# LSTM with residual on one core: the initial state's product goes into the x bank, and TensorE forms the second remainder of four of the eight weight parts with diagonal matrices

## The chip, the cores and the metric

The kernel runs on one core of a Trainium2 chip. The metric is the device time of one execution in microseconds (us); the median of three executions of the kernel before is 2270.43 us (2269.09 to 2270.66). Times of instructions come from one profiled execution, which took 2270.51 us as a whole and whose program spans 2268.2 us in the trace. All times below that say "at 44.78" are counted from the start of that span.

## What is computed

An LSTM layer runs over 512 time steps for a batch of 16, with 512 inputs and 512 hidden units; its output is added to the input.

```python
xW = jnp.einsum('ntd,dg->ntg', x, Wx) + b
def step(carry, xw_t):
    prev_h, prev_c = carry
    a = xw_t + prev_h @ Wh
    i = jax.nn.sigmoid(a[:, :Hdim])
    f = jax.nn.sigmoid(a[:, Hdim:2 * Hdim])
    o = jax.nn.sigmoid(a[:, 2 * Hdim:3 * Hdim])
    g = jnp.tanh(a[:, 3 * Hdim:])
    next_c = f * prev_c + i * g
    next_h = o * jnp.tanh(next_c)
    return ((next_h, next_c), next_h)
c0 = jnp.zeros_like(h0)
_, hs = jax.lax.scan(step, (h0, c0), jnp.swapaxes(xW, 0, 1))
x = x + jnp.swapaxes(hs, 0, 1)
```

x is (16, 512, 512), h0 is (16, 512), Wx and Wh are (512, 2048), all float32.

## The kernel before, in words

**Two stages.** A start prepares the weights and does step 0; then a loop (L519) does the 512 steps. All five engines' orders are written out by hand: each engine runs its instructions strictly in the order in which the program records them, and waits at the first one that is not ready. GpSimd (POOL) and SyncE (SP) issue the transfers, and their queues are in program order too.

**One step of the loop.** The list STEP_PE (L23) orders TensorE's work of a step: twelve products (q3aa to q3bb, 96 matmuls with 128x256 float16 moving data, line L210) and half of a projection of x two pairs of steps ahead (x0, x1: line L187, float32, 16 trace records). The list STEP (L24) orders the work of VectorE (DVE) and ScalarE (ACT): transposing the gates out of PSUM (turn, turno), folding two partial sums (fold, foldo), tanh and sigmoid, the new cell and the new h in float16 parts (p1, copy, p2, p2r, tile `parts`). The letters a and b stand for the two halves of the hidden units. The bank `gates` collects the products of one step and half; `seed` (L196) writes x's projection from bank `xb` into it before the products are added.

**The weights in parts.** The loop's products are float16. Therefore Wh is scaled by a power of two and split at the start into three float16 terms wq[0], wq[1], wq[2], in eight pieces n = 0 to 7 (piece n holds row block n // 2 and column half n % 2, 128x1024 each; pieces 0 to 3 belong to half a of the rows, 4 to 7 to half b). The scale needs the largest magnitude of each half: `bound` (L430) reduces it from the loaded weights, on DVE by a reduction, on ACT by an Abs with accumulation; `scales` (L444) turns it into powers of two. `split(n, k)` (L463) then makes five operations for each piece:

- k=0, wq[0] = scaled weights (ACT, L469; for pieces 6 and 7 DVE, L471)
- k=1, r1 = weights times scale minus wq[0] (DVE, L474)
- k=2, wq[1] = r1 (ACT, L478)
- k=3, r2 = r1 - wq[1] (DVE, L481)
- k=4, wq[2] = r2 times 4096 (ACT, L483)

**Step 0.** The initial state h0 is transposed to hT0 (L501) and multiplied with the float32 weights: `first_products` (L219), 64 matmuls of 128 columns into the gates banks, which have been seeded before; the loop's first pass runs them, and then the element work of step 0. Step 1 is the first that needs `parts` and the split weights; its first product is on the record at 44.78.

**Transfers.** SP issues the eight loads of Wh (L377), the eight of Wx (L388), then the rest of the first block of x and the second block (L151). POOL issues the four of h0 (L382) and then 24 for the first three pairs of steps of x (`load_first`, L156). A transfer's semaphore is used again eight transfers later, and the issue waits for the earlier landing. `turn_x` (L173) waits with one small copy (`seen`, L179) for the transfers of a group of pairs, and transposes x of one pair; before the first projection it waits for all three pairs.

**Banks.** There are four banks of gates (two halves, even and odd steps) and four of xb. TensorE first fills the gates with zeros (L407) and xb with the bias (L418); ACT copies the bias from xb[0] (L428).

Of the kernel before, what the change touches and what calls it, by code (L numbers as in the profile page):

```python
# [24 lines left out]
    "turn_a turno_a fold_a tanh_a foldo_a sig_a turn_b sigo_a scale_a mix_a fold_b "  # L25
    "tanh_b cell_a ctanh_a turno_b foldo_b sig_b p1_a sigo_b h_a copy_a mix_b p2_a "
    "scale_b cell_b rem_a ctanh_b p2r_a p1_b h_b copy_b p2_b rem_b p2r_b"
)


@with_exitstack
def lstm_residual(ctx: ExitStack, tc: tile.TileContext, x, h0, wx, wh, b, out):
# [68 lines left out]
    wq = [const.tile([P, NK, G * H], HP, tag=f"wq{i}", name=f"wq{i}") for i in range(3)]  # L101

    wx_j = wx_sb.rearrange("p k (g c j u) -> p k j g c u", g=G, c=NK, j=NJ)
    wh_j = wh_sb.rearrange(
        "p k (e g h c j u) -> p k e h j g c u", e=2, g=2, h=2, c=2, j=NJ
    )
    wq_j = [
        w.rearrange("p k (g h c j u) -> p k h j g c u", g=G, h=2, c=2, j=NJ) for w in wq
    ]
    bias = const.tile([P, G * P], FP, tag="bias", name="bias")  # L110
    mask = const.tile([P, S2], FP, tag="mask", name="mask")
    zero = const.tile([1, G * P], HP, tag="zero", name="zero")
    amax = const.tile([P, 5], FP, tag="amax", name="amax")
    top = const.tile([P, 2], FP, tag="top", name="top")
    bits = const.tile([P, 2, 2], FP, tag="bits", name="bits")
    sc = const.tile([P, 2, 4], FP, tag="sc", name="sc")
    S, RS, RS2, RSL = ([sc[:, h, i : i + 1] for h in range(2)] for i in range(4))


# [33 lines left out]
                        in_=x_j[j, :, s * XB + i0 * S2 + r : (s + 1) * XB : S2, c],  # L153
                    )

    def load_first(i1):  # L156
        xs[0] = xsp.tile([P, XP, P], FP, tag="xs", name="xs_0")
        for i in range(i1):
            for j in range(NJ):
                for r in range(S2):  # L160
                    p0 = j * Q + r * N
                    nc.gpsimd.dma_start(
                        out=xs[0][p0 : p0 + N, i].rearrange("p (c u) -> p c u", c=NK),
                        in_=x_j[j, :, i * S2 + r],
                    )
# [6 lines left out]

    def turn_x(q):  # L173
        s, i = divmod(q, XP)
        if i == 0 or q == FIRST:

            a, e = (0, FIRST) if q == 0 else (i, XP)
            seen = tmp.tile([P, XP, NK], FP, tag="seen", name=f"seen_{q}")
            nc.vector.tensor_copy(  # L179
                seen[:, a:e], xs[s].rearrange("p i (c u) -> p i c u", c=NK)[:, a:e, :, 0]  # L180
            )
        xT[q] = xtp.tile([P, NK, Q], FP, tag="xT", name=f"xT_{q}")
        nc.vector.transpose(xT[q].rearrange("p c m -> p (c m)"), xs[s][:, i])  # L183

    def project(q, c):
        for j in range(NJ):
            nc.tensor.matmul(  # L187
                xb[q % NXB][j * Q : (j + 1) * Q],
                lhsT=xT[q][:, c],
                rhs=wx_j[:, c, j],  # L190
                start=False,
                stop=False,
                skip_group_check=True,
            )

    def seed(t, h):  # L196
        nc.scalar.mul(  # L197
            gates[h][t % 2][:, :GU].rearrange("p (g u) -> p g u", g=G),
            xb[t // 2 % NXB].rearrange("p (g h u) -> p h g u", g=G, h=2)[:, h],
            mask[:, t % 2 : t % 2 + 1],  # L200
        )
# [14 lines left out]
                    skip_group_check=True,  # L216
                )

    def first_products(kh, h, hT):  # L219
        for cc in range(2):  # L220
            for e in range(2):
                for j in range(NJ):
                    nc.tensor.matmul(
                        gates[h][0][j * Q : (j + 1) * Q, (1 - e) * P : (2 - e) * P],
                        lhsT=hT[:, 2 * kh + cc],
                        rhs=wh_j[:, 2 * kh + cc, e, h, j],
                        start=False,
                        stop=False,
                        skip_group_check=True,
                    )  # L230


    gc = [state.tile([P, 2, 2 * N], FP, tag=f"gc{h}", name=f"gc{h}_init") for h in range(2)]
# [140 lines left out]
    for c in range(NK):  # L374
        for e in range(2):
            f = slice(e * GH, (e + 1) * GH)
            nc.sync.dma_start(out=wh_sb[:, c, f], in_=wh[c * P : (c + 1) * P, f])  # L377
    nc.vector.memset(zero, 0.0)
    nc.vector.memset(h_in, 0.0)
    nc.vector.memset(ones, 1.0)  # L380
    for j in range(NJ):
        nc.gpsimd.dma_start(  # L382
            out=h_in[j * Q : j * Q + N].rearrange("p (c u) -> p c u", c=NK), in_=h0_j[j]
        )
    load_first(FIRST)
    for c in range(NK):
        for e in range(2):
            nc.sync.dma_start(  # L388
# [38 lines left out]
                )  # L427
    nc.scalar.copy(bias, xb[0])  # L428

    def bound(i, c, on_act, f=slice(0, G * H)):  # L430
# [12 lines left out]

    def scales(h):  # L444


        nc.vector.tensor_reduce(
            top[:, h : h + 1], amax[:, 3 * h : 3 + 2 * h], mybir.AxisListType.X, ALU.max
        )
        t = top[:, h : h + 1].bitcast(I32)  # L450
        e, inv = bits[:, h, 0:1], bits[:, h, 1:2]
        nc.vector.tensor_scalar(
            inv.bitcast(I32), t, EXP, EXP, ALU.bitwise_and, ALU.bitwise_xor
        )
        nc.vector.tensor_scalar(e.bitcast(I32), t, EXP, None, ALU.bitwise_and)
        nc.vector.tensor_scalar(RS2[h], inv, 2.0**12, 0.5, ALU.mult, ALU.min)
        nc.vector.tensor_scalar(RS[h], inv, 2.0**13, 1.0, ALU.mult, ALU.min)
        nc.vector.tensor_scalar(S[h], e, 2.0**-14, 1.0, ALU.mult, ALU.max)
        nc.vector.tensor_scalar(RSL[h], RS[h], 1.0 / LO, None, ALU.mult)

    r1, r2 = {}, {}

    def split(n, k):  # L463
# [4 lines left out]
        if k == 0 and n < 6:  # L468
            nc.scalar.mul(f[0], w, RS2[c // 2])  # L469
        elif k == 0:  # L470
            nc.vector.tensor_scalar(f[0], w, RS2[c // 2], None, ALU.mult)  # L471
        elif k == 1:
            r1[n] = tmp.tile([P, GH], FP, tag="r1", name=f"r1_{n}")
# [3 lines left out]
        elif k == 2:  # L477
            nc.scalar.copy(f[1], r1[n])  # L478
        elif k == 3:
            r2[n] = tmp.tile([P, GH], FP, tag="r2", name=f"r2_{n}")  # L480
            nc.vector.tensor_tensor(r2[n], r1[n], f[1], ALU.subtract)  # L481
        else:
            nc.scalar.mul(f[2], r2[n], LO)  # L483

    NH = 2 * NK
    bound(0, 0, False)
    bound(1, 1, True, slice(0, GH))
    bound(2, 1, False, slice(GH, 2 * GH))
    scales(0)
    split(0, 0)  # L490
    split(0, 1)
    split(1, 0)
    for n in range(NH):
        if n == 1:
            bound(3, 2, False)
            bound(4, 3, True)
            scales(1)
        if n == 2:
            for q in range(FIRST):
                turn_x(q)  # L500
            nc.vector.transpose(hT0.rearrange("p c m -> p (c m)"), h_in)  # L501
            for q in range(2):
                for c in range(NK):
                    project(q, c)
        if n + 1 < NH:
            split(n + 1, 1)
        split(n, 2)
        split(n, 3)
        if n:
            split(n - 1, 4)  # L510
        if n + 2 < NH:
            split(n + 2, 0)
        if n == 5:
            for t in range(2):
                for h in range(2):
                    seed(t, h)
    split(NH - 1, 4)

    for t in range(T):  # L519
        s, ti = divmod(t, XB)  # L520
        q, half = divmod(t + 4, 2)
        if ti == 0:
            hist[s] = outp.tile([P, XP, NK, Q], FP, tag="hist", name=f"hist_{s}")

        for op in STEP_PE.split():
            if op[0] == "x":
                if q < NP:
                    project(q, 2 * half + int(op[1:]))
            elif t:
                products(t, int(op[1]), "ab".index(op[2]), "ab".index(op[3]))  # L530
            elif op[1] == "3":
                first_products("ab".index(op[2]), "ab".index(op[3]), hT0)

        for op in STEP.split():
            name, h = op.split("_")
            act(t, name, "ab".index(h))

        if t + 2 < T:
            seed(t + 2, 0)
        if t % 2:  # L540
            for h in range(2):
                unscale(t // 2, h)
            if q + 1 < NP:
                turn_x(q + 1)
        else:
            if t and q + 1 < NP:
                put_bias(q + 1)
            if t:
                residual(t // 2 - 1)
        if t + 2 < T:  # L550
            seed(t + 2, 1)
        if ti == 0 and s + 2 < NS:
            load_xs(s + 2)
# [29 lines left out]
```

## Time and profile before

| what | us |
|---|---|
| median of three executions | 2270.43 |
| the profiled execution | 2270.51 |
| its span in the trace | 2268.2 |
| busy in the span: TensorE matmuls / VectorE / ScalarE / GpSimd | 2234.5 / 1957.2 / 1839.7 / 131.1 |
| first product of step 1 (L210) | at 44.78 |
| first product of step 2, by the chain of waits | at 50.60 |
| one step later on, 2.62 of products and 1.72 of projection | 4.34 |
| stretch without a matmul before the first projection | 17.4 |

The profile's page lists for each engine busy time and share, then the span in 40 slices, the transfer queues, the chain of work that ended last, and groups of instructions (line, engine, operation, output and inputs, count, busy us, mean ns, idle time before them and what ended it). The timeline gives instructions in order of time: start in us, duration or extent of a merged run in us, engine, line, operation, output and inputs, count, and in brackets the engine's idle time before it and the releaser. The chain of waits in order of time gives start, length and what was on the chain. PE is TensorE, DVE VectorE, ACT ScalarE. A float32 matmul of the program leaves two matmul records.

### The profile page before, as it was taken

Reading aid. Unit: us, or ns where it says so; the run is one execution under the profiler, and the core shown is the slowest. Engines: PE = TensorE matmul, PEld = TensorE weight load, DVE = VectorE, ACT = ScalarE, POOL = GpSimd, SP = SyncE. Lnnn points to the kernel's source line nnn. Section 1 sums busy time; section 2 is a strip of 40 time slices with the busy share of each in tenths; the row PEclk is TensorE's granted clock in tenths of the full one; section 3 lists DMA queues with packets and bytes.
Section 4 is the critical chain, followed back from the end, with each engine's and each line's share of the span. In section 5 each row is a group of like instructions: output and inputs, shape, how many; then the busy total and the mean of one; then the engine's idle time right before and its main releaser. Section 6 shows DMA issues by size and latency. Waiting matters only on the chain.

```text
span 2268.2 us, 138001 instructions
## 1 busy us (share of the span) xinstructions
PE 2234.5 (99%) x57444; PEld 1466.8 (65%) x57444; DVE 1957.2 (86%) x11853; ACT 1839.7 (81%) x7959; POOL 131.1 (6%) x287
## 2 busy tenths in 40 slices
PE   6999999999999999999999999999999999999997
PEld 3666666666666666666666666666666666666665
DVE  7888888888888888888888888888888888888887
ACT  6888888888888888888888888888888888888887
POOL 2000000000000000000000000000000000000000
PEclk9999999999999999999999999999999999999999
DMA  5011111111111111111111111111111111111001
GB/s 166 16 22 23 16 17 16 22 22 19 17 17 19 22 22 16 17 17 22 23 18 16 17 20 23 22 16 17 16 23 22 19 16 17 20 22 21 15 9 17
DMA packets 297716, 50.93 MB, mean 22 GB/s; under 512 B 294593, under 2 KB 295041, under 8 KB 297089
## 3 DMA queue, kind: packets, MB, share of 16 engines
q1 hardware_dynamic: 295872, 41.85, 11.4%
q8 instruction: 450, 7.37, 1.4%
q14 instruction: 176, 1.44, 0.2%
q0 software_dynamic: 896, 0.23, 0.1%
q10 hardware_dynamic: 322, 0.04, 0.0%
HBM read 25.21 MB, written 16.78 MB: 19 GB/s over the span
## 4 chain that ended last, share of the span: by engine, by line
PE 97%; DMA 1%; DVE 1%; issue 0%; ACT 0%; POOL 0%; SPq 0%; POOLq 0%; DVEq 0%
PE gates L210 59%; PE xb L187 38%; DMA xs<-in_x_dram 1%; DVE r L481 0%; DMA h_in<-in_cond_dram 0%; DVE r L474 0%; ACT wq L483 0%; SPq L347 0%; POOL h_in L382 0%; DMA out_dram<-ob 0%; DVE wq L471 0%; DVE xT L183 0%; POOLq L578 0%; DVE pr L290 0%; POOL ob L359 0%
## 5 line engine op out<-in xcount | busy, mean ns | idle before, releaser
L210 PEld LDWEIGHTS <-parts 128*32 128x32 f16 x49056 | 1224.7, 96 | 442.2 <-DVE parts L306 306.0
L210 PE MATMUL gates<-wq,parts 128*32 128x256 f16 x49056 | 1427.4, 273 | 7.0 <-DVE parts L306 7.0
L187 PE MATMUL xb<-wx_sb,xT 128*32 128x512 f32 x8192 | 966.7, 593 | 17.4 <-DMA xs<-in_x_dram 17.4
L246 DVE STREAM_TRANSPOSE gt<-gates 128x192 f32<-128x192 f32 x1024 | 392.0, 383 | 216.2 <-PE gates L210 168.1
L187 PEld LDWEIGHTS xb<-wx_sb,xT 128*32 128x32 f32 x8192 | 235.4, 110 | 344.1 <-issue 340.3
L197 ACT ACTIVATE gates<-xb,mask 128x256 f32<-128x256 f32 x1024 | 451.3, 441 | 0.0
L280 ACT ACTIVATE gc<-pre 128x32 f32<-128x32 f32 x1022 | 234.6, 230 | 259.7 <-DVE pre L253 248.3
L288 ACT ACTIVATE os<-so,sc 128x32 f32<-128x32 f32 x1024 | 329.6, 322 | 16.7
L310 ACT COPY parts<-parts 128x32 f16<-128x32 f16 x1022 | 214.3, 210 | 132.2 <-DVE parts L306 132.2
L253 DVE SCALAR_TENSOR_TENSOR pre<-gt 128x96 f32<-128x96 f32 x1024 | 255.1, 249 | 0.0
L282 ACT ACTIVATE sif<-pre 128x64 f32<-128x64 f32 x1024 | 244.9, 239 | 0.0
L359 POOL TENSOR_TENSOR ob<-hb,xs 128x128 f32<-128x128 f32 x255 | 116.5, 457 | 2121.6 <-DVE hb L357 2039.4
L246 DVE STREAM_TRANSPOSE gto<-gates 128x64 f32<-128x64 f32 x1024 | 231.2, 226 | 0.0
L286 ACT ACTIVATE so<-preo 128x32 f32<-128x32 f32 x1024 | 227.0, 222 | 0.0
L298 ACT ACTIVATE tch<-gc 128x32 f32<-128x32 f32 x1024 | 226.8, 221 | 0.1
L320 DVE SCALAR_TENSOR_TENSOR parts<-rem,parts 128x32 f16<-128x32 f32 x1022 | 195.9, 192 | 35.5
L253 DVE SCALAR_TENSOR_TENSOR preo<-gto 128x32 f32<-128x32 f32 x1024 | 193.6, 189 | 17.5
L312 DVE SCALAR_TENSOR_TENSOR parts<-parts,hist 128x32 f16<-128x32 f16 x1022 | 193.3, 189 | 17.7
L290 DVE TENSOR_TENSOR pr<-sif,gc 128x64 f32<-128x64 f32 x1022 | 205.8, 201 | 0.0
L306 DVE TENSOR_TENSOR parts<-os,tch 128x32 f16<-128x32 f32 x1022 | 196.9, 193 | 0.0
L296 DVE TENSOR_TENSOR gc<-pr 128x32 f32<-128x32 f32 x1024 | 193.3, 189 | 0.0
L300 DVE SCALAR_TENSOR_TENSOR hist<-os,tch 128x32 f32<-128x32 f32 x1024 | 190.2, 186 | 0.3 <-ACT tch L298 0.3
(49 smaller groups left out, 740.1 us busy)
## 6 DMA issues: line engine op xcount, KB each, us to landing
xs<-in_x_dram SPq DMA_DIRECT2D x992, 16.0 KB, 2.1
out_dram<-ob SPq DMA_DIRECT2D x992, 16.0 KB, 1.6
wh_sb<-in_L_cond_Wh_dram SPq DMA_DIRECT2D x8, 512.0 KB, 7.8
wx_sb<-in_L_cond_Wx_dram SPq DMA_DIRECT2D x8, 512.0 KB, 11.7
out_dram<-ob SPq DMA_DIRECT2D x60, 8.0 KB, 1.5
xs<-in_x_dram SPq DMA_DIRECT2D x32, 10.0 KB, 2.3
xs<-in_x_dram POOLq DMA_DIRECT2D x24, 8.0 KB, 5.2
h_in<-in_cond_dram POOLq DMA_DIRECT2D x4, 8.0 KB, 6.0
```

Of the source, the lines that this page charges most:

```text
L187: nc.tensor.matmul(xb[q % NXB][j * Q : (j + 1) * Q], lhsT=xT[q][:, c], rhs=wx_j[:, c, j], start=False, stop=False, skip_group_check=True,)
L197: nc.scalar.mul(gates[h][t % 2][:, :GU].rearrange("p (g u) -> p g u", g=G), xb[t // 2 % NXB].rearrange("p (g h u) -> p h g u", g=G, h=2)[: ...
L210: nc.tensor.matmul(g[j * Q : (j + 1) * Q, :GU], lhsT=a[:, cc, k * N : (k + 2) * N], rhs=wq_j[i - 1][:, 2 * kh + cc, h, j], start=False, st ...
L246: nc.vector.transpose(gt.rearrange("p b m -> p (b m)"), gates[h][t % 2][:, b0 * Q : b1 * Q])
L253: nc.vector.scalar_tensor_tensor(pre.rearrange("p g (c n) -> p (g c) n", c=2), gt[:, :, (1 - t % 2) * N : (2 - t % 2) * N], 1.0 / LO, gt[: ...
L280: nc.scalar.activation(gc[h][:, 0], v["pre", h][:, 0], AF.Tanh)
L282: nc.scalar.activation(new("sif", t, h, [P, 2, 2 * N]), v["pre", h][:, 1:3], AF.Sigmoid)
L286: nc.scalar.activation(new("so", t, h, [P, 2 * N]), v["preo", h][:, 0], AF.Sigmoid)
L288: nc.scalar.mul(new("os", t, h, [P, 2 * N]), v["so", h], S[h])
L290: nc.vector.tensor_tensor(new("pr", t, h, [P, 2, 2 * N]), v["sif", h], gc[h], ALU.mult)
L298: nc.scalar.activation(new("tch", t, h, [P, 2 * N]), gc[h][:, 1], AF.Tanh)
L310: nc.scalar.copy(slots(t, h, 2), slots(t, h, 0))
```

## The change

Only the start and the first pass of the loop change; STEP_PE, STEP and the loop from step 1 stay as they are.

- **Order.** A list START replaces the nested order of the start and the loop's step 0. Each entry is one operation: b (bound), S (scales), hT, H (first product with row block c), xT (turn_x), P.q.c (project), seed, q1/q2/q3 (the three float16 terms; the suffix s is ACT, v is DVE), r1/r2, d1/d2/d3 (diagonal matmuls), and step 0's element operations. The loop begins at step 1.
- **h0's product.** `first_products` writes to xb[0], beside x's projection, as 32 matmuls of 256 columns instead of 64 of 128 into the gates; step 0's seeds then read the sum.
- **The second remainder on TensorE.** For pieces 0, 1, 2 and 4 (BY_PE, which names the gates banks used) r1 and r2 are not made on DVE. Instead DVE makes wq[1] directly in float16 (one operation), and TensorE makes the remainder in two gates banks: +scale diagonal times the float32 weights (d1, `rows`), minus-one diagonal times wq[0] (d2) and times wq[1] (d3, `neg16`), each as two matmuls of 512 columns with a full 128x128 stationary operand. ACT reads the two banks and writes wq[2] (q3).
- **The diagonal.** POOL makes `neg` with a memset and an affine_select, after h0's transfers and the first eight of x, ahead of the other sixteen of x. DVE copies it to `neg16`, ahead of the transposition of h0 and of the bounds, and makes `rows` at the end of each `scales`. In the built program POOL's library-configuration instruction, which was ahead of the first residual addition (L359), stands between the memset and the affine_select; on DVE the copy to `neg16` is the first instruction after the initial memsets.
- **Bounds.** Block 0 is bounded by ACT as a whole, block 1 by DVE in two pieces, blocks 2 and 3 by ACT; the maxima have eight columns, cleared first.
- **x.** The three first pairs are waited for one by one.

```diff
+BY_PE = {0: 1, 1: 0, 2: 1, 4: 0}
+START = (
+    "hT b.0.s H.0 b.1a.v b.1b.v H.1 S.0 q1.1.v d1.1 q1.2.s q1.3.v b.2.s q2.1.v d1.0 "
+    "q1.0.v b.3a.s r1.3 d2.1 d2.0 b.3b.s H.2 q2.0.v q2.3.s d3.1 S.1 q3.1.s d3.0 H.3 "
+    "xT.0 r2.3 q1.4.s d1.4 q1.7.s xT.1 q2.4.v P.0.0 q3.3.s r1.7 d2.4 q1.5.s d3.4 P.0.1 "
+    "q2.2.v q3.0.s P.1.0 r1.5 q2.7.s P.1.1 q3.4.s r2.7 P.0.2 q1.6.s P.1.2 q2.5.v q3.7.s "
+    "P.0.3 xT.2 r1.6 d1.2 seed.0.0 seed.0.1 turn_a q2.6.s turno_a turn_b fold_a turno_b "
+    "d2.2 fold_b tanh_a foldo_a sig_a foldo_b r2.6 d3.2 tanh_b sigo_a sigo_b sig_b "
+    "P.1.3 q3.2.s mix_a mix_b P.2.0 cell_a cell_b r2.5 scale_a ctanh_a ctanh_b scale_b "
+    "P.2.1 seed.1.0 seed.1.1 p1_a h_a h_b copy_a p1_b q3.5.s p2_a rem_a rem_b p2r_a "
+    "q3.6.v copy_b p2_b p2r_b seed.2.0 seed.2.1"
+)
...
+    def first_products(c):
+        for e in range(2):
+            for j in range(NJ):
+                nc.tensor.matmul(
+                    xb[0][j * Q : (j + 1) * Q, (1 - e) * GU : (2 - e) * GU],
+                    lhsT=hT0[:, c],
+                    rhs=wh_j[:, c, e, j],
...
-    load_first(FIRST)
+    load_first(0, 1)
+    nc.gpsimd.memset(neg, 0.0)
+    nc.gpsimd.affine_select(
+        out=neg, in_=neg, compare_op=ALU.not_equal, fill=-1.0, base=0,
+        pattern=[[-1, P]], channel_multiplier=1,
+    )
+    load_first(1, FIRST)
...
+    nc.vector.tensor_copy(neg16, neg)
...
+        nc.vector.tensor_scalar(rows[h], neg, RS[h], -1.0, ALU.mult, ALU.mult)
...
+        if op[0] == "d":
+            i = int(op[1])
+            for m in range(2):
+                g = slice(m * G * P, (m + 1) * G * P)
+                nc.tensor.matmul(
+                    gates[m][BY_PE[n]],
+                    lhsT=rows[c // 2] if i == 1 else neg16,
+                    rhs=w[:, g] if i == 1 else f[i - 2][:, g],
+                    start=(i == 1),
+                    stop=(i == 3),
+                    skip_group_check=True,
+                )
+        elif op == "q3" and n in BY_PE:
+            for m in range(2):
+                cast(on_act, f[2][:, m * G * P : (m + 1) * G * P], gates[m][BY_PE[n]], LO)
+        elif op == "q2" and n in BY_PE:
+            nc.vector.scalar_tensor_tensor(f[1], w, RS[c // 2], f[0], ALU.mult, ALU.subtract)
+        elif op == "q1":
+            cast(on_act, f[0], w, RS2[c // 2])
...
+    hist[0] = outp.tile([P, XP, NK, Q], FP, tag="hist", name="hist_0")
+    for op in START.split():
+        start(*op.split("."))
+    load_xs(2)
-    for t in range(T):
+    for t in range(1, T):
```

More of the change, by code (lines that the diff above doesn't have):

```diff
@@ L103, in lstm_residual @@
     wx_j = wx_sb.rearrange("p k (g c j u) -> p k j g c u", g=G, c=NK, j=NJ)
-    wh_j = wh_sb.rearrange(
-        "p k (e g h c j u) -> p k e h j g c u", e=2, g=2, h=2, c=2, j=NJ
-    )
+    wh_j = wh_sb.rearrange("p k (e g c j u) -> p k e j g c u", e=2, g=2, c=NK, j=NJ)
     wq_j = [
@@ L112, in lstm_residual @@
     zero = const.tile([1, G * P], HP, tag="zero", name="zero")
-    amax = const.tile([P, 5], FP, tag="amax", name="amax")
+    amax = const.tile([P, 8], FP, tag="amax", name="amax")
     top = const.tile([P, 2], FP, tag="top", name="top")
@@ L116, in lstm_residual @@
     sc = const.tile([P, 2, 4], FP, tag="sc", name="sc")
+    neg = const.tile([P, P], FP, tag="neg", name="neg")
+    neg16 = const.tile([P, P], HP, tag="neg16", name="neg16")
+    rows = [const.tile([P, P], FP, tag=f"rows{h}", name=f"rows{h}") for h in range(2)]
     S, RS, RS2, RSL = ([sc[:, h, i : i + 1] for h in range(2)] for i in range(4))
@@ L154, in load_xs, with load_first @@
                     )
-    def load_first(i1):
-        xs[0] = xsp.tile([P, XP, P], FP, tag="xs", name="xs_0")
-        for i in range(i1):
+    def load_first(i0, i1):
+        if i0 == 0:
+            xs[0] = xsp.tile([P, XP, P], FP, tag="xs", name="xs_0")
+        for i in range(i0, i1):
             for j in range(NJ):
@@ L174, in turn_x @@
         s, i = divmod(q, XP)
-        if i == 0 or q == FIRST:
-            a, e = (0, FIRST) if q == 0 else (i, XP)
+        if i == 0 or q <= FIRST:
+            a, e = (i, i + 1 if q < FIRST else XP)
             seen = tmp.tile([P, XP, NK], FP, tag="seen", name=f"seen_{q}")
@@ L217, in products @@
                 )
[L219 to L230, printed above, removed]
+    def first_products(c):
[5 more added lines that the diff above has]
+                    rhs=wh_j[:, c, e, j],
+                    start=False,
+                    stop=False,
+                    skip_group_check=True,
+                )
     gc = [state.tile([P, 2, 2 * N], FP, tag=f"gc{h}", name=f"gc{h}_init") for h in range(2)]
@@ L378, in lstm_residual @@
     nc.vector.memset(zero, 0.0)
+    nc.vector.memset(amax, 0.0)
     nc.vector.memset(h_in, 0.0)
@@ L384, in lstm_residual @@
         )
-    load_first(FIRST)
+    load_first(0, 1)
+    nc.gpsimd.memset(neg, 0.0)
+    nc.gpsimd.affine_select(
+        out=neg,
+        in_=neg,
+        compare_op=ALU.not_equal,
+        fill=-1.0,
+        base=0,
+        pattern=[[-1, P]],
+        channel_multiplier=1,
+    )
+    load_first(1, FIRST)
     for c in range(NK):
@@ L428, in lstm_residual, with bound @@
     nc.scalar.copy(bias, xb[0])
-    def bound(i, c, on_act, f=slice(0, G * H)):
+    nc.vector.tensor_copy(neg16, neg)
+    def bound(piece, on_act):
+        c = int(piece[0])
+        i = 2 * c + (piece[-1] == "b")
+        f = slice(0, 2 * GH) if len(piece) == 1 else slice((i % 2) * GH, (i % 2 + 1) * GH)
         w = wh_sb[:, c, f]
@@ L447, in scales @@
         nc.vector.tensor_reduce(
-            top[:, h : h + 1], amax[:, 3 * h : 3 + 2 * h], mybir.AxisListType.X, ALU.max
+            top[:, h : h + 1], amax[:, 4 * h : 4 * h + 4], mybir.AxisListType.X, ALU.max
         )
@@ L459, in scales, with cast, split @@
         nc.vector.tensor_scalar(RSL[h], RS[h], 1.0 / LO, None, ALU.mult)
+        nc.vector.tensor_scalar(rows[h], neg, RS[h], -1.0, ALU.mult, ALU.mult)
     r1, r2 = {}, {}
-    def split(n, k):
+    def cast(on_act, out, in_, scale):
+        if on_act:
+            nc.scalar.mul(out, in_, scale)
+        else:
+            nc.vector.tensor_scalar(out, in_, scale, None, ALU.mult)
+    def split(op, n, on_act):
         c, e = divmod(n, 2)
@@ L467, in split @@
         f = [q[:, c, (1 - e) * GH : (2 - e) * GH] for q in wq]
[L468 to L473, printed above, removed]
+        if op[0] == "d":
[8 more added lines that the diff above has]
+                    stop=(i == 3),
+                    skip_group_check=True,
+                )
+        elif op == "q3" and n in BY_PE:
[5 more added lines that the diff above has]
+            cast(on_act, f[0], w, RS2[c // 2])
+        elif op == "r1":
+            r1[n] = tmp.tile([P, GH], FP, tag="r1", name=f"r1_{n}", bufs=4)
             nc.vector.scalar_tensor_tensor(
@@ L476, in split @@
             )
-        elif k == 2:
-            nc.scalar.copy(f[1], r1[n])
-        elif k == 3:
+        elif op == "q2":
+            (nc.scalar.copy if on_act else nc.vector.tensor_copy)(f[1], r1[n])
+        elif op == "r2":
             r2[n] = tmp.tile([P, GH], FP, tag="r2", name=f"r2_{n}")
@@ L482, in split, with start @@
         else:
[L483 to L500, printed above, removed]
-            nc.vector.transpose(hT0.rearrange("p c m -> p (c m)"), h_in)
[L502 to L517, printed above, removed]
-    for t in range(T):
+            cast(on_act, f[2], r2[n], LO)
+    def start(op, a="", b=""):
+        if op == "b":
+            bound(a, b == "s")
+        elif op == "S":
+            scales(int(a))
+        elif op == "hT":
+            nc.vector.transpose(hT0.rearrange("p c m -> p (c m)"), h_in)
+        elif op == "xT":
+            turn_x(int(a))
+        elif op == "H":
+            first_products(int(a))
+        elif op == "P":
+            project(int(a), int(b))
+        elif op == "seed":
+            seed(int(a), int(b))
+        elif "_" in op:
+            name, h = op.split("_")
+            act(0, name, "ab".index(h))
+        else:
+            split(op, int(a), b == "s")
+    hist[0] = outp.tile([P, XP, NK, Q], FP, tag="hist", name="hist_0")
[3 more added lines that the diff above has]
+    for t in range(1, T):
         s, ti = divmod(t, XB)
@@ L528, in lstm_residual @@
                     project(q, 2 * half + int(op[1:]))
-            elif t:
+            else:
                 products(t, int(op[1]), "ab".index(op[2]), "ab".index(op[3]))
-            elif op[1] == "3":
-                first_products("ab".index(op[2]), "ab".index(op[3]), hT0)
         for op in STEP.split():
@@ L545, in lstm_residual @@
         else:
-            if t and q + 1 < NP:
+            if q + 1 < NP:
                 put_bias(q + 1)
-            if t:
-                residual(t // 2 - 1)
+            residual(t // 2 - 1)
         if t + 2 < T:
```

## The prediction

> **What bounds the kernel now.** I read the page first, then the chain of waits in order of time, then the timeline of the first 50 us.
>
> ```profile
> span 2268.2 us, 138001 instructions
> PE 97%; DMA 1%; DVE 1%; issue 0%; ACT 0%; POOL 0%; SPq 0%; POOLq 0%; DVEq 0%
> ```
>
> TensorE is 97% of the chain. The loop is bound by it, and the change leaves the loop alone. So only what lies ahead of TensorE's unbroken run can move. The chain of waits (start, length, what) shows where that begins:
>
> ```profile
> 3.23 6.58 DMA h_in<-in_cond_dram
> ...
> 21.48 5.21 DMA xs<-in_x_dram
> ...
> 26.96 0.17 DVE seen L179
> ...
> 40.00 2.35 DVE r L481 x2
> ...
> 42.37 1.06 ACT wq L483
> ...
> 44.78 4.10 PE gates L210 x93
> 48.88 1.72 PE xb L187 x16
> 50.60 2.62 PE gates L210 x93
> 53.22 1.72 PE xb L187 x15
> ```
>
> From 3.23 to 26.7 POOL's transfers are the chain, each waiting for an older landing; DVE then sits in `seen`. From 27 to 42.4 it is mostly DVE's remainders, at 44.78 step 1 begins. Its products take 4.10 where step 2's take 2.62: the granted clock is 0.67 between 44.8 and 48.9, after TensorE was idle from 42.0 to 44.8. From 48.88 on a step is 2.62 + 1.72 = 4.34 without a gap. **The measure of the change is therefore one number: when step 1's products end, now 48.88.** Every microsecond there is one in the total.
>
> **Part 1: when the diagonal is ready.** In the new order DVE's first instruction after the memsets is the copy to neg16, which waits for POOL. Behind it in DVE's queue stand hT, the bounds and scales, so also TensorE's H and d, and ACT's q1. POOL reaches the memset after its eighth transfer of x:
>
> ```profile
> 10.09 0.51 POOL L162 DMA_DIRECT2D xs<-in_x_dram  x1 [0.59 <-DMA h_in<-in_cond_dram]
> 56.48 0.45 POOL L359 TENSOR_TENSOR ob<-hb,xs 128x128 f32<-128x128 f32 x1 [34.48 <-DVE hb L357]
> ```
>
> 10.09 + 0.51 = 10.6. The memset I put at 0.2 (DVE's of that shape took 0.17), the affine_select at 0.3, between nothing and the 0.45 of POOL's addition of that shape. Without anything else neg is ready at 11.1.
>
> But the configuration instruction now stands between the two:
>
> ```profile
> L359 POOLq MODIFY_POOL_CONFIG  x2: 37/37/37, 22.0 to 22.0; - x2
> ```
>
> Its two records take 37 ns each; the first compute operation behind them came 34.4 us later, when DVE's hb was ready, so this trace can hide a code load of any length up to that. The Trainium skill (GPSIMD Engine Reference, Instruction dispatch) says that the first call to freshly loaded GpSimd code pays a load of about 6 us, which shows as no instruction, between this very instruction and the call. By the row neg is ready at 11.1 and the total comes out 9.6 lower than before; by the rule at 17.1, and 3.6 lower (sum below). No row is near, so the page's price is the middle: I take 7, somewhat more, since the transfer engines are at a share of 0.97 from 10.1 to 27.4. The ends are 0 and 13.5: POOL's 8 KB transfers take a median of 5.2 us to land here, SP's 10 KB ones mostly later 2.3, and 6 x 5.2 / 2.3 = 13.5 (an estimate). **neg at 18.1.**
>
> The other sixteen x transfers stand behind the load in POOL's queue: pair 1 is issued from 18.1 to 22.2 and landed by about 27.2, with the 5.0 that such transfers take now; its transposition is due at about 29.8. Pair 0, which is waited for alone, is issued before and landed at 16. So the waits of 26.7 go, and nothing of x is late next; the last Wx load lands at about 28, and its projection comes after that.
>
> **Part 2: from neg to the end of step 1 on TensorE.** Prices, from these rows:
>
> ```profile
> 1.18 1.88 PE L407 MATMUL gates<-zero 1*128 1x512 f16 x4 [1.18 <-DVE zero L378]
> 3.00 7.05 PE L418 MATMUL xb<-brow,ones 1*32 1x256 f32 x64
> 27.45 3.34 PE L187 MATMUL xb<-wx_sb,xT 128*32 128x512 f32 x13 [17.41 <-DMA xs<-in_x_dram]
> 29.13 6.84 PE L187 MATMUL xb<-wx_sb,xT 128*32 128x512 f32 x56
> 36.54 3.70 PE L223 MATMUL gates<-wh_sb,hT 128*32 128x128 f32 x128 [0.57 <-ACT gates L197]
> ```
>
> In steady running four L187 records (four column tiles) start every 0.43 (16 in 1.72), so one projection of a row block, eight records, is 0.86.
> - P: ten of these, 8.6, as many as before.
> - H: the same multiplications as L223's 3.70 in wider pieces; 16 groups of four records at 0.43 x 256/512 = 0.215: 3.4.
> - d1: eight float32 matmuls of 512 columns over all 128 columns of the array. Four tiles of 32 columns side by side are the nearest row, two records of 0.43: 0.86 each, 6.9. Below this nothing speaks for a price; above, weight loads that do not overlap would add some 0.2 each (L407's of 128 columns took 0.13 to 0.20), 1.6 in all. I take the row.
> - d2, d3: 16 float16 matmuls of 512 columns. L407's four took 0.43 apart (half clock); at full clock half of that: 3.4.
> - Step 1: 2.6.
>
> Sum 24.9. Half clock: L187's records started 0.85 apart until 30.4 and 0.43 after, 3 us after TensorE had begun. H.0 will start after an idle time again, so I add 2.3, between 1.7 (3.4 us at half clock) and 3.4 (twice that). neg16 and hT ahead of H.0: 0.4. Together 27.6.
>
> VectorE over the same stretch: eight scalar_tensor_tensor of 1.19 (rows 1.17 to 1.20 on the chain), four r2 of 1.14, five casts, of which four fall before h's parts, of 0.67, two bounds of 1.14, two scales of 0.85, x's transpositions 0.8, step 0's group 2.2: about 24, on the heels of TensorE's 25.0 up to step 1, where before eight r1 and eight r2 alone took 18.7. ScalarE reads a 128x512 bank in 0.59 (L428), two for 1.05 from SBUF: no difference. Three engines so close hand over to each other without slack; I add 0.6 (nothing to 2). DVE's q1 casts beside POOL's issues are not in this trace; pair 1's slack of 2.6 covers them.
>
> Clock in step 1: TensorE is busy until step 1, so the 4.10 becomes 2.62; this is in the sum.
>
> **Sum.** 18.1 + 27.6 + 0.6 = 46.3 against 48.88: 2.6 us less. Span 2265.6; with the 2.3 around it (2270.5 - 2268.2) **2267.9 us**. The profiled execution is within 0.1 of the median shown, so this stands for the median too. The effect is 0.11%; a measurement here tells from no change about 0.2%, 4.5 us.
>
> **Second rule weighed: the clock.** The Trainium skill (TensorE: Matmul & The Clock Gate, Part 1) says that about 3.4 us of activity bring the full clock. L418's row speaks against a plain reading: 64 records in 7.05 us, 0.44 for four of 256 columns, twice the 0.215 above, to its end; a stationary operand with one row of 128 did not bring it, though TensorE was busy from 1.2 to 10.1. (The clock column shows 1.00 there; the spacing tells it.) A diagonal matrix is one live weight per column. By the rule d1 to d3 run at full clock, 10.3; by that row at half, 20.6. I take the rule, because all 128 rows are in use, as in L187, which did reach it.
>
> **Rivals.**
> - *The load costs nothing* (the code is already there, as two 37 ns records suggest): neg at 11.1, step 1 ends at 39.3, 9.6 less: **2260.9**. Against it: the rule, and that no row shows the configuration followed at once by its first call. Then x's remaining transfers of block 0, issued by SP until about 41, may cost step 1's `seen` some tenths.
> - *The diagonals stay at half clock* (slower): 10.3 more between H.1 and d3.2 on TensorE, -2.6 + 10.3 = 7.7 more: **2278.2**. It decides the sign as soon as more than 2.6 us of the 10.3 run at half clock. For it L418; against it L187.
> - *The load takes 13.5 beside full transfers*: 6.5 more than taken, 3.9 more than before: **2274.4**.
>
> **Chances.** Forecast 0.55 (load 6 to 9, clock as taken; its own range 2265.5 to 2270.5), load free 0.17, half clock 0.15, long load 0.13. Faster by over 0.2% (under 2265.9): 0.17 and about a quarter of the forecast's case, 0.31. Slower by over 0.2%: 0.15 and 0.05 of the long load, 0.20. Within: 0.49. The range takes in the free load and the long load and leaves the half clock out: 2260 to 2275.
>
> **What would show it.** POOL's timeline: a gap between neg's memset and affine_select of about 7 with nothing in it; neg16 on DVE ending a long wait at about 18; H.0 right after it. d1 records 0.43 apart once the clock is up, their weight loads beside them. Step 1's first L210 at about 43.7, and 2.62 for it. The prediction is wrong if neg comes before 13 or after 23, if d1 takes over 2 us for a pair, or if the loop's 4.34 changes.

## The result, and the profile after

| | before | changed |
|---|---|---|
| median (lowest to highest), 5 runs each, us | 2270.43 (2269.09 to 2272.09) | 2261.51 (2261.34 to 2262.27) |
| span of the profiled execution, us | 2268.2 | 2259.7 |
| step 1's products end, us | 48.88 | 40.35 |
| span less that end, us | 2219.32 | 2219.35 |

The ratio is 0.9961, 95% interval 0.9949 to 0.9974: faster by 0.4%, and the interval leaves out 1. The last two rows are the whole account. Step 1's products end 8.53 us earlier, the span is 8.5 us shorter, and what follows them took the same time. (The median moved 8.9, 0.4 more: the time outside the span was 1.8 us instead of 2.3.)

The page of the changed kernel, its span and the chain's shares by engine:

```profile
span 2259.7 us, 137960 instructions
...
PE 99%; issue 0%; DVE 0%; SPq 0%; DMA 0%; POOLq 0%; POOL 0%
```

The chain of waits in order of time (start, length, engine, tile and line) shows why the share is now 99%:

```profile
10.08 1.66 issue
11.74 3.64 PE xb L241 x32
15.38 4.72 PE gates L514 x12
20.10 1.00 PE xb L241 x16
21.10 0.97 PE gates L514 x4
...
24.98 0.99 PE xb L206 x8
25.98 0.97 PE gates L514 x4
26.95 5.29 PE xb L206 x48
...
37.73 2.62 PE gates L229 x96
40.35 1.72 PE xb L206 x16
```

L241 is H, h0's product; L514 the diagonal matmuls; L206 the projections of x; L229 a step's products. From 11.74 on each piece begins where the one before it ends. TensorE never waits again, neither for VectorE's remainders nor for x, and step 1's products take 2.62 at once, where before they took 4.10. So what sets the time now is when TensorE starts, and how much it has to do until 37.73.

It starts when the diagonal is ready. GpSimd's timeline (start, length, engine, line, operation, tiles):

```profile
9.51 1.02 POOL L181 DMA_DIRECT2D xs<-in_x_dram  x2 [0.67 <-DMA h_in<-in_cond_dram]
10.52 0.22 POOL L405 MEMSET neg<- 128x128 f32 x1
10.82 0.29 POOL L406 TENSOR_SCALAR_AFFINE_SELECT neg<-neg 128x128 f32<-128x128 f32 x1
11.30 2.52 POOL L181 DMA_DIRECT2D xs<-in_x_dram  x5 [0.19 <-issue]
```

and the instructions of line 406:

```profile
L406 POOLq MODIFY_POOL_CONFIG  x2: 37/37/37, 10.7 to 10.7; - x2
```

The configuration instruction is there, between the memset and the affine_select, as the prediction had it. The 7 us behind it are not: the affine_select starts at 10.82. The diagonal is ready at 11.11, not at 18.1.

### The profile page after: what moved, and what is told of

The parts are those of the page before. It is cut to its first block, busy times and chain, and to the rows that moved or that the text cites. A ratio compares the mean times of both kernels' runs of the same rounds, so it can differ in the third digit from the quotient of the medians.

```text
span 2259.7 us, 137960 instructions
## 1 busy us (share of the span) xinstructions
PE 2245.1 (99%) x57412; PEld 1515.9 (67%) x57412; DVE 1950.6 (86%) x11857; ACT 1833.1 (81%) x7960; POOL 131.1 (6%) x289
## 4 chain that ended last, share of the span: by engine, by line
PE 99%; issue 0%; DVE 0%; SPq 0%; DMA 0%; POOLq 0%; POOL 0%
PE gates L229 59%; PE xb L206 39%; PE gates L514 1%; PE xb L448 0%; PE xb L241 0%; SPq L365 0%; PE gates L437 0%; DMA out_dram<-ob 0%; POOLq L624 0%; POOL ob L377 0%; DVE parts L338 0%; DVE gt L264 0%; DVE ob L377 0%; DVE parts L330 0%; DVE zero L396 0%
## 5 line engine op out<-in xcount | busy, mean ns | idle before, releaser
L229 PEld LDWEIGHTS <-parts 128*32 128x32 f16 x49056 | 1264.8, 96 | 397.8 <-DVE parts L324 301.2
L229 PE MATMUL gates<-wq,parts 128*32 128x256 f16 x49056 | 1428.1, 273 | 4.2 <-DVE parts L324 4.2
L206 PE MATMUL xb<-wx_sb,xT 128*32 128x512 f32 x8192 | 967.4, 592 | 0.0
L206 PEld LDWEIGHTS xb<-wx_sb,xT 128*32 128x32 f32 x8192 | 240.6, 110 | 320.0 <-issue 317.2
```

Source lines behind the costliest of these rows:

```text
L206: nc.tensor.matmul(xb[q % NXB][j * Q : (j + 1) * Q], lhsT=xT[q][:, c], rhs=wx_j[:, c, j], start=False, stop=False, skip_group_check=True,)
L229: nc.tensor.matmul(g[j * Q : (j + 1) * Q, :GU], lhsT=a[:, cc, k * N : (k + 2) * N], rhs=wq_j[i - 1][:, 2 * kh + cc, h, j], start=False, st ...
```

## The experiments

Each run has, besides its time, two numbers to read: when H.0 starts, and when step 1's products end. One table for all, in us; the ratio is to runs of the kernel before taken beside it (their medians: 2270.43 for the changed kernel, 2270.11, 2270.16 or 2270.31 for the others).

| kernel | H.0 starts | step 1's products | span | median | ratio [95%] |
|---|---|---|---|---|---|
| changed | 11.74 | 37.73 to 40.35 | 2259.7 | 2261.51 | 0.9961 [0.9949, 0.9974] |
| e1_neg_late | 22.47 | 47.96 to 50.58 | 2270.0 | 2272.58 | 1.0010 [1.0001, 1.0020] |
| e9_broadcast | 19.89 | 45.64 to 48.26 | 2267.8 | 2270.36 | 1.0001 [0.9992, 1.0011] |
| e10_iota | 11.92 | 38.06 to 40.68 | 2260.1 | 2261.85 | 0.9965 [0.9952, 0.9978] |
| e2_no_diag | 11.52 | 40.97 to 45.44 | 2264.8 | 2266.80 | 0.9986 [0.9977, 0.9996] |
| e3_x_at_once | 11.79 | 41.61 to 44.23 | 2263.8 | 2266.14 | 0.9984 [0.9975, 0.9994] |
| e5_filler (from before) | none | 45.58 to 48.20 | 2268.6 | 2269.83 | 0.9998 [0.9989, 1.0008] |
| e4_neg_early | 11.11 | 37.87 to 40.49 | 2259.9 | 2260.92 | 0.9961 [0.9948, 0.9973] |
| e6_three | 11.71 | 37.23 to 40.26 | 2259.8 | 2262.67 | 0.9969 [0.9957, 0.9980] |
| e7_early_four | 10.81 | 36.82 to 39.44 | 2258.9 | 2261.00 | 0.9958 [0.9945, 0.9972] |
| e8_early_three | 10.75 | 36.10 to 39.13 | 2258.6 | 2260.66 | 0.9959 [0.9947, 0.9972] |

In all of them but e5 the span less the end of step 1's products is 2219.4 to 2219.6, so the measure that the prediction chose holds throughout. (In e5 it is 2220.4; the 0.9 more lies behind the last step's products.)

### Does the whole start hang on the diagonal? (e1)

```diff
     load_first(0, 1)
-    nc.gpsimd.memset(neg, 0.0)
-    nc.gpsimd.affine_select(out=neg, in_=neg, ...)
     load_first(1, FIRST)
+    nc.gpsimd.memset(neg, 0.0)
+    nc.gpsimd.affine_select(out=neg, in_=neg, ...)
```

> The changed kernel, with one move on GpSimd: neg's memset and affine_select stand after all 24 transfers of x instead of after the first eight. neg is then ready at about 22.5 instead of 11.1. Theory (the whole start hangs on neg through VectorE's first copy, and nothing between neg and step 1 has slack): step 1's first product moves from 37.7 by the same 11.4, to about 49.1, total about 2273, slower than the kernel before. Rival (something else, h0 or the weights, was late as well, or the engines catch up): it moves by 9 or less, total under 2270.5.

The chain of waits of e1:

```profile
10.05 12.42 issue
22.47 3.37 PE xb L241 x32
...
47.96 2.62 PE gates L229 x96
```

The copy of neg on VectorE moved from 11.14 to 21.87, by 10.73, and step 1's products by 10.23. Nearly every microsecond on the diagonal is one in the time. So a load of 7 us there would have cost nearly 7 us, and its price was the number that decided the forecast.

### Is there such a load on this chip at all? (e9, e10)

```diff
-    nc.gpsimd.memset(neg, 0.0)
+    nc.gpsimd.partition_broadcast(neg, nil)        # e9; nil: 128 zeros, set by VectorE
+    nc.gpsimd.iota(neg, pattern=[[0, P]], ...)     # e10
```

> neg is first filled by GpSimd's partition_broadcast of a zero row (memset by VectorE) instead of GpSimd's memset; the affine_select behind it and everything else is as in the changed kernel. Theory (the load that the prediction priced is paid only by operations whose code is not yet on GpSimd, and a memset, an addition and an affine_select are not such, while a broadcast across partitions is): a stretch of about 6 us (5 to 13.5) with no instruction on GpSimd ahead of the broadcast, neg ready near 17 instead of 11.1, H.0 near 17.7, step 1's products end near 46.5, time near 2267.5; this would also say that the prediction's sum was right but for the load. Rival (in this program no GpSimd code is ever loaded behind the start): the broadcast takes a few tenths, neg at 11 to 11.6, time 2261.3 to 2262.3, as the changed kernel.

> As e9, with an iota of zeros in the memset's place. Both theories leave open which side an iota falls on: a load shows as 5 us or more with no instruction ahead of it and a time near 2267; without one neg is ready near 11.2 and the time is 2261.3 to 2262.3.

GpSimd's timeline in e9:

```profile
10.14 0.51 POOL L181 DMA_DIRECT2D xs<-in_x_dram  x1 [0.37 <-DMA h_in<-in_cond_dram]
18.47 0.43 POOL L407 PARTITION_BROADCAST neg<-nil  x1 [7.82 <-issue]
18.97 0.29 POOL L408 TENSOR_SCALAR_AFFINE_SELECT neg<-neg 128x128 f32<-128x128 f32 x1
```

and the configuration instruction of its line 407:

```profile
L407 POOLq MODIFY_POOL_CONFIG  x2: 37/37/37, 10.9 to 10.9; - x2
```

The same two records of 37 ns, and then 7.5 us in which GpSimd does nothing that the profile shows. In e10 they stand there too, and the timeline goes on at once:

```profile
10.67 0.26 POOL L405 IOTA neg<- 128x128 f32 x1
11.00 0.29 POOL L406 TENSOR_SCALAR_AFFINE_SELECT neg<-neg 128x128 f32<-128x128 f32 x1
```

So a wait of the priced size exists, ahead of the broadcast; memset, affine_select and iota do not have it. That it is a load of code, and that the code of the other three is always in GpSimd's memory, is the natural reading, but not shown: the trace names nothing in the gap, and with one broadcast in the run, a wait that every broadcast has looks the same. With this wait the change loses its whole gain: e9's ratio to the kernel before is 1.0001. The theory's time for e9, 2267.5, was 2.9 too low: the gap ahead of the broadcast was 7.8 instead of 6, so the products end at 48.26 instead of 46.5, and the median lies 0.8 above the profiled execution's 2269.54.

### What do the diagonal matmuls bring? (e2)

```diff
-BY_PE = {0: 1, 1: 0, 2: 1, 4: 0}
+BY_PE = {}
```

with the order of START rewritten for eight remainders of each kind on VectorE.

> The changed kernel without its diagonal matmuls: pieces 0, 1, 2 and 4 get r1 and r2 on VectorE and q2 on ScalarE as before, in the new order; all else as changed. Theory (TensorE's 10.3 us of diagonals replace 4.6 us of VectorE, which had about 1.5 us of idle time after neg): VectorE bounds the start, step 1 starts 3 to 4.6 us later, at 40.7 to 42.3, perhaps with 1.4 more for half clock in its products; total 2264.5 to 2267.5. Rival (the gain comes from the order and the x waits alone): no later than 38.7, total under 2262.5.

The end of e2's chain of waits:

```profile
39.68 1.14 DVE r L538
40.81 0.11 DVE parts L324
40.97 4.47 PE gates L229 x96
45.44 1.72 PE xb L206 x16
```

Step 1 waits for VectorE's last remainder, and its products run at half clock for 3.41 of their 4.47, after TensorE had idled for 2.15 ahead of them. Against the changed kernel its end is 5.09 later: 3.24 for the later start, 1.85 for the slower products, nearly all of it the clock. Against the kernel before it is 3.44 earlier: that much the rest of the change brings in this order of START (h0's product early, x taken in by pairs and the new order together; this run does not split them).

### What does taking x by pairs bring? (e3)

```diff
-        if i == 0 or q <= FIRST:
+        if i == 0 or q == FIRST:
...
-            a, e = (i, i + 1 if q < FIRST else XP)
+            a, e = (0, FIRST) if q == 0 else (i, XP)
```

> The changed kernel, but VectorE waits once for the transfers of all three first pairs of x, as before the change. The last of them landed at 27.5 in the changed kernel. Theory (VectorE and TensorE are both full): VectorE stands from 21.4 to about 27.7, step 1 starts 5 to 6 us later, at about 43; total about 2267. Rival (VectorE has slack behind TensorE, which loses only the wait in front of its first projection, 24.98 to 28.1): 3 us later, total about 2264.6. If x's waits were no part of the gain: no change.

e3's chain of waits:

```profile
28.71 0.30 DVE xT L202
29.01 1.18 DVE wq L526
30.20 0.04 issue
30.24 0.59 PE gates L514 x2
30.83 5.29 PE xb L206 x48
```

VectorE stood still for 5.83 us until the third pair had landed, at 27.30, and the work queued behind it came later: r2 of piece 3, then wq[1] of pieces 4 and 2 (L526) for TensorE's d3. TensorE's long run of projections starts at 30.83 instead of 26.95: 3.88, all of which arrives at step 1. The cost lies between the two expectations: TensorE could make up part of the 5.83 by work that did not need VectorE.

### Is the clock ahead of step 1 by itself worth something? (e5)

The kernel before, with 12 float32 matmuls of zeros put between the start's work and step 1, so that TensorE does not idle there:

```diff
+        if t == 0:
+            for c in range(3):
+                for j in range(NJ):
+                    nc.tensor.matmul(xb[3][...], lhsT=blank, rhs=wx_j[:, c, j], start=False, ...)
```

> The kernel before, with 12 more float32 matmuls on TensorE between step 0's last projection and step 1: an all-zero stationary operand of 128 rows times Wx, added to xb[3], some 2.6 us that fill the idle stretch from 42.0 to 44.8. Theory (step 1's products took 4.10 instead of 2.62 because the idle stretch halved the clock, and a zero operand in all rows counts as activity): step 1's products take 2.62, total 1.2 to 1.5 us less, about 2269.1. Rival (only live operands count): 4.10 as before, total unchanged at 2270.4.

The chain of waits of e5:

```profile
27.86 9.93 PE xb L188 x64
...
43.00 2.58 PE xb L539 x24
45.58 2.62 PE gates L211 x96
48.20 1.72 PE xb L188 x16
```

The products take 2.62 instead of 4.10. But they start 0.8 later, since in this execution the clock rose at 33.66 (30.41 in the one of before), the projections ended later, and the filler had to follow them. Of 1.48 us, 0.68 was left, and the medians do not tell it from nothing.

Whether the filler kept the clock up is not shown. The granted clock changes only on a grid of 3.41 us (last section). In the kernel before, the step of the grid ahead of the drop, 40.65 to 44.07, had TensorE busy for 1.30 of it. In e5 the grid lies elsewhere: in its steps from 40.49 and from 43.90 the needed matmuls alone, without the filler, keep TensorE busy for about 2.5 and 1.9, and e6 kept its clock after a step with 1.6. So what e5's theory and its rival say of zeros is not decided.

### What bounds the changed kernel now? (e4, e7, e6, e8)

e4 puts neg's two instructions ahead of all of GpSimd's transfers. e7 also takes a fourth pair of x by GpSimd's queue. e6 is the changed kernel with piece 4 of Wh back on VectorE and ScalarE, and e8 is e7 with e6's three parts.

```diff
-BY_PE = {0: 1, 1: 0, 2: 1, 4: 0}
+BY_PE = {0: 1, 1: 0, 2: 1}        # e6, e8
-    FIRST = 3
+    FIRST = 4                      # e7, e8
```

> neg's memset and affine_select are put ahead of h0's and x's transfers on GpSimd, which idles from 0.45 to 1.58 us there. Theory (the instruction needs no load of code, and with e1 the start hangs on when neg, and then h0, is there): neg ready near 1.5, neg16's copy no longer waits for it, hT is copied at h0's landing near 9.7-9.9, H.0 starts near 10.2 (11.74 in the changed kernel), step 1's products end up to 1.5 us earlier, near 38.9; the time falls by 0.5 to 1.5 us, to 2260.0-2261.0, less than the shift because seen_3 may then wait for xs_0's transfers (last landing near 42.9). Rival (a load of GpSimd's code was there but lay hidden under the transfers that stand ahead of it): as the first instruction of its kind it takes some 7 us at the front, h0's transfers issue 7 us later, H.0 starts near 17, and the time is about 2267.

> As e4, and a fourth pair of row blocks of x comes by GpSimd's queue instead of SyncE's, so that the last of xs_0 lands earlier. If in e4 the wait for xs_0 takes back part of the shift, this gives it again: H.0 near 10.2, step 1's products end near 38.9, no idle of TensorE behind them, time near 2260.0. If e4 lost nothing there, e7 equals e4 within 0.5 us.

> One of the four parts (piece 4 of Wh) goes back to VectorE and ScalarE. TensorE is relieved of three groups of four diagonal matmuls, 3 x 0.97 = 2.9 us; VectorE gets one remainder of 1.14 us more, ScalarE two rounds of 0.59 in place of PSUM reads. Theory (TensorE alone bounds the start: it ran without idle from 11.74): step 1 up to 2.9 us earlier, near 34.8, the time near 2258.6-2260. Rival (VectorE is as late as TensorE: it had only 1.4 us idle from 11.14 to 36.96): step 1 starts between 37.0 and 38.2, TensorE idles ahead of it, and the time is 2261-2262, no different from the changed kernel.

> e7 with e6's three parts. If TensorE bounds the start, both gains add: H.0 near 10.2, step 1 some 4 us earlier than in the changed kernel, near 33.5, time near 2257-2259. If VectorE is as late, e8 equals e7 within 0.5 us.

In e4 the affine_select comes 1 us after the span's start, with nothing but memsets ahead of it:

```profile
0.74 0.20 POOL L400 MEMSET neg<- 128x128 f32 x1 [0.29 <-POOLq L615]
1.02 0.29 POOL L401 TENSOR_SCALAR_AFFINE_SELECT neg<-neg 128x128 f32<-128x128 f32 x1
1.59 2.17 POOL L411 DMA_DIRECT2D h_in<-in_cond_dram  x4 [0.28 <-DVE mask L429]
```

So no load was hidden under transfers either. H.0, however, started at 11.11, not at 10.2: h0's last transfer landed at 10.58 in this execution (9.64 in the changed kernel's), and hT waits for it. The expectation of 10.2 was a miss, as h0 takes the diagonal's place at once. The 0.63 that H.0 gained was then lost in e4's next pieces:

```profile
11.11 3.64 PE xb L241 x32
14.75 5.49 PE gates L514 x12
20.24 1.00 PE xb L241 x16
```

The second piece is 5.49 instead of 4.72. The clock rose at 16.72 here, 5.6 us after H.0, where it rose after 4.1 in the changed kernel. In e7 H.0 starts at 10.81, the clock rises 4.1 later, and the whole 0.9 arrives. TensorE did not idle behind step 1 in either, so the wait for xs_0 that e4's expectation feared did not come.

In e6 TensorE gets an idle stretch again. Its timeline, at step 1:

```profile
37.23 3.03 PE L229 MATMUL gates<-wq,parts 128*32 128x256 f16 x96 [2.27 <-DVE parts L324]
```

Taking 2.9 us off TensorE moved step 1's start by 0.5, and 2.27 turned into a wait for VectorE; the products then take 3.03 and end only 0.09 earlier than in the changed kernel. That is the rival's case: at four parts the two engines are as late as each other. e8 says the same with H.0 early: 1.32 us of waiting for VectorE. The medians of e4, e7 and e8 are 0.5 to 0.9 us under the changed kernel's 2261.51, that of e6 1.2 above. These differences are about 0.05% or less, and each is known only against the kernel before, so none is called better than the changed kernel. e6's six executions fall in two groups of three, 2261.5 to 2261.8 and 2263.6 to 2264.0; the profiled one is of the faster group. A spell at half clock in step 1, as in e2, would cost about 1.7 (an estimate: half of its 3.41) and could come from the new idle stretch, but no trace of the slower group is on record.

## Why the prediction came out as it did

The forecast was 2267.9, the time 2261.51. It fell within the range, near its lower end, in the case that the prediction gave 0.17; the case it held likeliest did not come. That the number fit is owed to the width of the range, 15 us, and not to the mechanism: the gain was 8.9 where 2.6 was forecast, and by the prediction's own sign, neg before 13, it was wrong.

**The bound.** Right. The loop's step is still 2.62 + 1.72, and the move of step 1's end is the move of the span.

**The step that failed: "I take 7", the load of GpSimd's code behind the configuration instruction.** It measured 0. The prediction read its one row correctly: in the kernel before, the trace allowed any load from nothing to 34.4 us. It then took the page's price as the middle. The Trainium skill (GPSIMD Engine Reference, Instruction dispatch) has about 6 us for the first call of *freshly loaded* code; e9 shows a gap of that kind, 7.8 us beside the transfers, and e10 and the changed kernel show the same configuration instruction without one. The error was to take the instruction for the sign of a load. Nothing in the trace before told the two cases apart: its four memsets ran ahead of the configuration, and its first addition 34.4 us behind it. The other reading had only the rival's chance, and no part in the middle.

**TensorE's work.** The price of a float32 diagonal, two records of 0.43, was right; the nearest row, four column tiles side by side, was the right one to take. From TensorE's timeline, d2 of two pieces (float16) and d1 of one (float32):

```profile
19.07 1.03 PE L514 MATMUL gates<-wq,neg 128*128 128x512 f16 x4
...
23.00 1.98 PE L514 MATMUL gates<-wh_sb,rows 128*128 128x512 f32 x4
```

The chain, which counts to the next piece's start, gives that float32 group 1.91, where four records of 0.43 are 1.72; the four float16 ones take 0.97, where 0.86 is due; a single row block's projection takes 0.99, where 0.86 is due, but six in a run take 5.29, 0.13 more than 6 x 0.86. So the records cost what was taken; each group of them costs 0.11 to 0.2 on top, however long it is. What sets the groups apart is the switch between tiles of 32 columns and the full array. TensorE's weight loads (PEld) and matmuls (PE) at such a switch, and in the loop between a step's products and a projection, where the type changes but not the width (the timeline gives a matmul's own start, up to 0.2 ahead of the chain's, as matmuls overlap):

```profile
20.03 0.59 PEld L241 LDWEIGHTS xb<-wh_sb,hT 128*32 128x32 f32 x16 [0.42 <-issue]
20.03 1.07 PE L241 MATMUL xb<-wh_sb,hT 128*32 128x256 f32 x16
...
40.06 0.24 PEld L206 LDWEIGHTS xb<-wx_sb,xT 128*32 128x32 f32 x8
40.16 1.90 PE L206 MATMUL xb<-wx_sb,xT 128*32 128x512 f32 x16
```

In the loop the loads of the next piece start 0.10 ahead of its matmuls, under the products, and nothing is added. At the switch the first load starts with the matmul: it is not hidden. One such load takes 0.1, that of a float32 diagonal 0.19, which is about the size of what is added. The prediction had weighed loads that do not overlap, 1.6 for d1, and left them out; within a group they do overlap, at a switch they do not. (It read L407's loads as 0.13 to 0.20; they took 0.10 to 0.15.) Eleven groups lie ahead of step 1. TensorE took 25.99 from H.0 to step 1; P, H and d are 22.3, the half clock 2.03, and the 1.66 left over is put down to the switches. The sum had nothing for them.

**Handovers and neg16.** 0.6 was taken for three engines handing over to each other; TensorE waited 0. From neg to H.0 0.4 was taken; it was 0.63.

**The clock.** 2.3 was taken for the start at half clock; 2.03 measured (H.0 and H.1 took 3.64 instead of 1.72, and a little of d1). That the size fit is in part luck of the grid: in e4 the rise came 1.55 later, counted from H.0. The second rule weighed held: the diagonals, one live weight in each column, keep the clock up. From 15.8 on they run at full speed, though the grid's step from 15.80 to 19.22 holds nothing but diagonals, and the rival that held them at half clock is refuted. The step's 4.10 became 2.62, as the sum had it.

Put together: -2.6 as forecast, -7.0 for the load, +1.66 left over for the switches, -0.6 for the handovers, +0.23 for neg16, -0.27 for the clock is -8.6; measured -8.53.

**The rivals.** "The load costs nothing" came, at 2261.5 instead of its 2260.9; the difference is the term for switches. Its fear that step 1 would wait for x's transfers did not. The longer load did not come here; e9 shows what 7.8 us would have meant: no gain.

## What to carry to other kernels

Before pricing a one-time cost that the profile cannot show, ask which operations can pay it at all; and where such a term decides most of the effect, keep it as a case of its own and not as the middle of an estimate (here plain operations of GpSimd, a memset, an affine_select, an iota, took 0.2 to 0.3 us, and a partition broadcast stood behind a gap of 7.8). When engines share a start-up, moving work to the idle one pays until they are equally late (e6), and then the moment at which all of them may begin is what is left (e1, e7). Where a sum of matmul records is made, count the switches of tile width beside the records.

## What the runs showed of the hardware

- The gap on GpSimd: 7.8 us of idleness ahead of a partition_broadcast (e9), none ahead of an affine_select (changed) or an iota (e10), behind two configuration records of 37 ns in all three.
- Each group of matmuls between two switches from tiles of 32 columns to the full array, or back, took TensorE 0.11 to 0.2 us more than its records (changed kernel); between products and projections of the loop, both on 32 columns, nothing was added.
- The rise of the clock is not tied to the start of the work. In six executions with the same instructions from H.0 to step 1 it rose 2.96 (e1), 3.47 (e9), 4.06 (changed), 4.11 (e7), 4.36 (e10) and 5.61 us (e4) after H.0, and that stretch took 25.49 us in e1 and 26.76 in e4. The record of the granted clock shows why: its spells at half speed in the midst of a run are 3.41 (before) or 6.83 and 3.41 (e2) long, steps of one grid that runs on its own. Busy times of TensorE in single steps of that grid (without the bias's matmuls) fit these traces throughout: the clock rose after steps with 2.66 (e2), 2.72 (e8) or more, not yet after 2.20 (e4) or 2.38 (e5); it fell after steps with 1.30 (before), 1.26 or 1.13 (e2), and stayed up after 1.59 (e6) or 1.81 (e3). So the rise waits for the first step that is busy enough, and where H.0 falls in the grid is chance. The Trainium skill (TensorE: Matmul & The Clock Gate, Part 1) calls the window free-running, with a moment of rise that varies by 0.5 us to either side; here it varied by 2.7 in all. So a single profile of this start is good to about 1.3 us (half of 2.7), and smaller differences between two profiles, as those of e4, e6 and e7 above, hold for these executions alone.
- The bias's matmuls, whose stationary operand has a single row, ran at half clock to their end, 7.01 us of them without a break (changed kernel), while the diagonals over 128 rows kept the full clock. Whether zeros over 128 rows do is open (e5).
- The last of h0's four transfers of 8 KB landed between 9.51 and 10.58 us in kernels that issue them within 0.2 us of the same time. The three latest landings are those of e4, e7 and e8; whether neg's place has to do with it was not tried.
